# A pre-norm decoder layer with a sorted mixture of experts: another order of work at its start and in its last sorting

## The chip, the cores and the metric

The kernel runs on one core of a Trainium2 chip, as one program with one launch. The metric is device time in microseconds (us), the median of several runs. The core has a matrix engine (PE, TensorE), a vector engine (DVE), a scalar engine (ACT), a general engine (POOL, GpSimd) and SyncE (SP), which here only starts transfers. Each engine takes its instructions strictly in the order of the program; they wait for one another through semaphores. Transfers started by SP, ACT and POOL share 16 DMA engines. All data is fp32.

## The reference

There are 8 batches of 512 tokens with 256 features. Three blocks follow one another, each with a layer norm ahead and a residual add behind:

```python
# 1: attention as a causal circular convolution, 16 heads of 16
z = softmax(einsum('bse,he->bsh', x, W_A) * 16 ** -0.5, axis=1)
out[i] = sum over j <= i of z[(i - j) % S] * v[j]      # per head; then W_O and b_O
# 2: causal cross-attention: keys from norm(x), values and queries from ctx, scores / 16
# 3: mixture of experts: 2 shared experts of width 128 for all tokens,
#    16 routed experts of width 64, each token goes to the top 2 of a softmax router
out = shared(x) + sum over the 2 chosen e of weight_e * wd[e] @ (silu(wg[e] @ x) * (wu[e] @ x))
```

## The kernel before

**Batches and steps.** Work on a batch is cut into named steps, closures which issue their instructions when called. `steps_front` makes the first block's input side: `tr0 tr1` transpose the normed x, `z` makes the softmax over time (for batch 0 from two products, else by transposing), writes it to DRAM (`zd`) and loads it back as four shifted tiles `T`, 1 MB each; `v0 v1` make the values in time-reversed order, `q0 q1 cv0 cv1` the cross-attention's operands, `bias` adds b_O to x on POOL. `steps_back` makes the convolution (`c00` to `c11`, products `pc`), the projection, the second norm, scores, attention, third norm, and then the router: `lg` and `rt` (top 2), `rk` (the rank of each token in its expert: where its row goes), and eight sends `sd0` to `sd7`, indirect DMAs on POOL which write the token's row to its place in a DRAM table `xg` (line 584). `steps_shared` holds the shared experts: `h0 h1` (line 610, PSUM tag `gu` with three buffers) and `d0 d1` (line 627). A hand-written list `ORDER` interleaves the steps of the batches b-1 (names with `-`), b, b+1 (`+`) and b+2 (`++`).

**Routed experts.** The batches form two groups, 0 to 5 and 6 to 7. When a group's rows have been sent, each expert's rows lie together in `xg`, padded to tiles of 128 rows. `tiled` and `tabled` work out on DVE and PE which expert and which rows each tile has. The tiles are worked on in quads of four: group 0 has 16 quads, group 1 has 8. For a quad q, `fetch` loads the tiles' rows on SP (line 721), `pick` copies the expert's up and gate weights on ACT and loads the down weights `wdn`, `turn` transposes the rows (line 756; its first DVE operation, line 748, waits for the fetch), `hidden` makes the two products (line 775), `down` the third (line 791) and scales it, and four `put`s scatter the rows to a DRAM table `yg` by an indirect DMA on POOL (line 814). The fetch of quad 0 waits for the group's last send.

**Joining.** For each batch, `keep` reloads the saved x (group 0 only), `take` loads 2 x 512 KB from `yg` (line 858, on SP), and `join` adds both on DVE (line 867) and stores the output on SP. `yg` is one tensor in DRAM: the scatters to it are declared independent of each other, but a `take` waits for the scatters ahead of it in the program, and a scatter that the program has behind a `take` waits for this take.

**Order.** The order of issue comes from the program: `merged` spreads several lists evenly over each other, and `idle(n)` puts n empty steps in. The scheduler of the framework then moves instructions a little within each engine's queue. In iteration b=6 the first steps of group 0's tiles and quads 0 to 4 are spread over the iteration, in iteration 7 quads 5 to 12. Behind the loop come the last sorting (rank and sends of batch 7), the rest of group 0's quads and the shared experts of batch 7, in an order written out by hand; then group 1's quads, merged with the six joins of group 0 (`old`), and last the two joins of group 1. `warm` issues a product that nobody reads (128 x 128 by 512), behind each `hidden` and `down` of group 1.

Of the kernel before, what the change touches and what calls it, by code (L numbers as in the profile page):

```python
# [8 lines left out]
F32 = mybir.dt.float32  # L9
# [7 lines left out]
P = 128  # L17
B, S, D = 8, 512, 256
NT = S // P
KC = D // P  # L20
H, HD = 16, 16
NE = 16
MR = 64
# [49 lines left out]
def decoder_layer(ctx: ExitStack, tc: tile.TileContext, x, ctxT, waT, wvT, woT, bo, wkT, xwv, wqT, wr, wg, wu, wd, out):  # L73
    nc = tc.nc
# [16 lines left out]

    load_x(0)

    ident = const.tile([P, P], F32, name="ident")
    make_identity(nc, ident)
    mask = const.tile([P, P], F32, name="mask")
# [4 lines left out]
    nc.gpsimd.iota(rank_i, pattern=[[0, NT], [-1, NE]], base=NE, channel_multiplier=0)  # L101
    rank = const.tile([P, NT, NE], F32, name="rank")
    nc.vector.tensor_copy(rank, rank_i)
    ones = const.tile([P, P], F32, name="ones")
    nc.gpsimd.memset(ones, 1.0)

    before = const.tile([P, P], F32, name="before")
    nc.gpsimd.affine_select(out=before, in_=ones, compare_op=ALU.is_gt, fill=0.0, base=0, pattern=[[1, P]], channel_multiplier=-1)
# [163 lines left out]
    def steps_front(b):  # L272
        s = st[b]
# [11 lines left out]
        def zsoft():  # L285
            if b == 0:

                pz = ps.tile([P, 512], F32, tag="mm", bufs=3, name=f"pz{b}")
                for k in range(KC):
                    nc.tensor.matmul(pz[:H, :], wa_sb[:, k, :], s["xnT"][:, k, :], start=(k == 0), stop=(k == KC - 1))  # L290
                z = pz[:H, :].rearrange("h (i t) -> h i t", t=P)
            else:

                pz = ps.tile([P, 512], F32, tag="tr", bufs=2, name=f"pz{b}")
                for i in range(NT):
                    nc.tensor.transpose(pz[:H, i * P:(i + 1) * P], s["z"][:, i, :], ident)
                z = pz[:H, :].rearrange("h (i t) -> h i t", t=P)[:, :, ::-1]
            nm = small.tile([H, 1], F32, tag="znm", name=f"znm{b}")
            nc.vector.tensor_reduce(nm, pz[:H, :], AX.X, ALU.max, negate=True)
# [3 lines left out]
            nc.scalar.activation(zp[:, P:].rearrange("h (i t) -> h i t", t=P), z, AF.Exp, bias=nm, accum_out=zs)  # L303
            zr = small.tile([H, 1], F32, tag="zr", name=f"zr{b}")
            nc.vector.reciprocal(zr, zs)
            nc.vector.tensor_scalar_mul(zp[:, P:], zp[:, P:], zr)
            zd = dram.tile([H, ZW], F32, tag="zd", name=f"zd{b}")
            nc.sync.dma_start(out=zd, in_=zp)
            s["T"] = []
            for q in range(H // HPT):  # L310

                t = sb.tile([P, HPT, S], F32, tag="T", bufs=4, name=f"T{b}_{q}")
                src = bass.AP(zd.tensor, zd.offset + q * HPT * ZW + 1, [[1, P], [ZW, HPT], [1, S]])
                s["T_ins"] = nc.sync.dma_start(out=t, in_=src).ins
                s["T"].append(t)
            if 2 <= b < 6:
                for g in range(2):
                    put_blanks(g, b - 2, s["T_ins"])
# [316 lines left out]
        steps += [down(cp) for cp in range(2)]  # L635
        return named("h0 h1 d0 d1", steps)

    def warm(n, name, behind):

        p = ps.tile([P, 512], F32, tag="mm", bufs=3, name=f"warm_{name}")  # L640
        with tc.issue_after(behind):
            for _ in range(n):
                nc.tensor.matmul(p, ident, wgu_r[:, 0, 0, :512], start=True, stop=True)


    def tiled(g):

# [63 lines left out]
    def steps_routed(g):  # L711
# [53 lines left out]
        def hidden(q):  # L765
            def f():
                wgu, xT = G["wgu", q], G["xT", q]

                p = ps.tile([P, 2, QT // 2, P], F32, tag="gu", bufs=3, name=f"pgu{g}_{q}")
                for n in range(2):  # L770
                    for j in range(QT // 2):
                        for k in range(KC):
                            for o in range(2):
                                i = 2 * j + o
                                last = nc.tensor.matmul(p[o * MR:(o + 1) * MR, n, j, :], wgu[:, i, n, k, :], xT[:, k, i, :], start=(k == 0), stop=(k == KC - 1)).ins  # L775
                if g:
                    warm(1, f"h{q}", last)
                h = sb.tile([P, QT // 2, P], F32, tag="rh", bufs=2, name=f"rh{g}_{q}")
                nc.scalar.activation(h, p[:, 0], AF.Tanh, scale=0.5)
                nc.vector.scalar_tensor_tensor(h, h, 1.0, p[:, 0], ALU.add, ALU.mult)  # L780
                nc.vector.scalar_tensor_tensor(h, h, 0.5, p[:, 1], ALU.mult, ALU.mult)  # L781
                G["h", q] = h
            return f

        def down(q):
            def f():
                h, wdn = G["h", q], G["wdn", q]
                py = [ps.tile([P, QT // 2, D], F32, tag="gu", bufs=3, name=f"py{g}_{q}_{o}") for o in range(2)]
                for j in range(QT // 2):
                    for o in range(2):  # L790
                        last = nc.tensor.matmul(py[o][:, j, :], h[o * MR:(o + 1) * MR, j, :], wdn[o * MR:(o + 1) * MR, j, :], start=True, stop=True).ins  # L791
                if g:
                    warm(1, f"d{q}", last)
                if g == 0:
                    y = [sb.tile([P, D], F32, tag="y", bufs=8, name=f"y{g}_{q}_{i}") for i in range(QT)]
                else:
                    y = sb.tile([P, QT, D], F32, tag="xT", bufs=4, name=f"y{g}_{q}")
                    y = [y[:, i, :] for i in range(QT)]
                for o in range(2):
                    for j in range(QT // 2):  # L800
                        i = 2 * j + o
                        w = G["w", q][:, i:i + 1]
                        if j == 0:
                            nc.scalar.mul(y[i], py[o][:, j, :], w)  # L804
# [36 lines left out]
    def steps_join(g):  # L841
# [3 lines left out]
        def keep(bi):  # L845
            def f():
                b = GROUPS[g][bi]
                x = sb.tile([P, NT, D], F32, tag=("oT", "xn1", "ctxT")[bi % 3], bufs=1, name=f"xj{b}")
                nc.sync.dma_start(out=x, in_=st[b]["kept"])
                G["xj", bi] = x  # L850
            return f
# [30 lines left out]
    for n in FRONT.split():  # L882
        if n == "q0":
            make_qk()
        fronts[0][n]()
    for f in ln[1]:
        f()

    def iteration(b):
        x = dict(backs[b])  # L890
        if b > 0:
            x |= {f"-{n}": f for n, f in [*shared[b - 1].items(), *backs[b - 1].items()]}
        if b + 1 < B:
            x |= {f"+{n}": f for n, f in fronts[b + 1].items()}
        if b + 2 < B:
            x |= named("++l0 ++l1", ln[b + 2])

        ends = b == GROUPS[0][-1]
        order = ORDER.split() + (["rk", *[f"sd{i}" for i in range(8)]] if ends else [])
        return [x[n] for n in order if n in x and not (b == GROUPS[1][0] and n[:3] in ("-rk", "-sd"))]  # L900

    def flat(x):
        return [f for y in x for f in y]

    for b in range(B):
        if b + 2 < B:
            load_x(b + 2)
        now = iteration(b)
        if b == 6:
            now = merged(now, first[:1] + idle(4) + first[1:-1] + idle(12) + first[-1:] + flat(quads[:5]))  # L910
        elif b == 7:
            now = merged(now, flat(quads[5:13]))
        for f in now:
            f()
        if b == 0:
            load_blank()
        if b == 1:
            load_experts()
    last, sh = backs[B - 1], shared[B - 1]
    gap = flat(quads[13:])  # L920
    q = len(gap) // 4
    for f in [last["rk"], *gap[:q], sh["h0"], *[last[f"sd{i}"] for i in range(8)], *gap[q:2 * q], sh["h1"], first1[0],
              *gap[2 * q:3 * q], *first1[1:-1], *gap[3 * q:], sh["d0"], sh["d1"], first1[-1]]:
        f()
    keeps, takes, joins = steps_join(0)
    n = len(keeps)
    old = [keeps[0], takes[0], keeps[1], takes[1]]
    for i in range(n):
        old.append(joins[i])
        if i + 2 < n:  # L930
            old += [keeps[i + 2], takes[i + 2]]
    keeps, takes, joins = steps_join(1)
    for f in merged(flat(quads1), old):
        f()
    for f in [*keeps, *takes, *joins]:
        f()
# [54 lines left out]
```

## Time and profile before

| | |
|---|---|
| median of 3 runs | 583.35 us (580.09 to 584.81) |
| the profiled execution | 585.7 us; span of its instructions 584.0 us |
| busy: PE, DVE, ACT, POOL | 518.3, 373.7, 191.5, 228.1 us |
| mean granted PE clock | 0.966 |
| moved by DMA | 107.67 MB, mean 184 GB/s |

In the profile a line gives the start in us, the duration, the engine, the source line with the operation, what it writes and reads (partitions x elements), the number of instructions merged, and in brackets the engine's idle time ahead of it and what ended it. `128*64` ahead of a shape is the part of the PE array in use. An fp32 product shows as two records, a transpose as one. SPq, ACTq and POOLq are these engines' queues when they start transfers. A line of the waits reads: who waited for what: us in total, times, longest.

In time, the iterations of the loop fill about 30 to 478 us; the rank and the sends of batch 7 come from 478 to 493, group 1's quads from there to 562, and the last joins until 584.

### The profile page before, as it was taken

Reading aid. Unit: us, or ns where it says so; the run is one execution under the profiler, and the core shown is the slowest. Engines: PE = TensorE matmul, PEld = TensorE weight load, DVE = VectorE, ACT = ScalarE, POOL = GpSimd, SP = SyncE. Lnnn points to the kernel's source line nnn. Section 1 sums busy time; section 2 is a strip of 40 time slices with the busy share of each in tenths; the row PEclk is TensorE's granted clock in tenths of the full one; section 3 lists DMA queues with packets and bytes.
Section 4 is the critical chain, followed back from the end, with each engine's and each line's share of the span. In section 5 each row is a group of like instructions: output and inputs, shape, how many; then the busy total and the mean of one; then the engine's idle time right before and its main releaser. Section 6 shows DMA issues by size and latency. Waiting matters only on the chain.

```text
span 584.0 us, 10066 instructions
## 1 busy us (share of the span) xinstructions
PE 518.3 (89%) x3176; PEld 334.8 (57%) x3176; DVE 373.7 (64%) x1289; ACT 191.5 (33%) x483; POOL 228.1 (39%) x258
## 2 busy tenths in 40 slices
PE   3989989999999999999999679999899899898830
PEld 1537626666665675764765356775566665664510
DVE  4327848768768787877976476547756575453553
ACT  2233313322224233224222326444344342452310
POOL 3300302530540630621434402444576457564550
PEclk9999999999999999999999889999999999998985
DMA  8491090671391392184182357955556323778797
GB/s 272 143 396 34 11 347 23 200 279 58 139 348 59 111 324 110 66 305 192 48 293 98 109 153 193 313 165 199 164 171 207 101 88 123 197 231 298 229 327 251
DMA packets 64108, 107.67 MB, mean 184 GB/s; under 512 B 8902, under 2 KB 37580, under 8 KB 63954
## 3 DMA queue, kind: packets, MB, share of 16 engines
q1 hardware_dynamic: 51672, 83.87, 43.4%
q0 software_dynamic: 7680, 16.87, 8.0%
q10 hardware_dynamic: 4704, 6.29, 3.2%
q8 instruction: 25, 0.41, 0.3%
q14 instruction: 27, 0.22, 0.1%
HBM read 82.35 MB, written 34.38 MB: 200 GB/s over the span
## 4 chain that ended last, share of the span: by engine, by line
PE 54%; DMA 16%; DVE 11%; issue 6%; POOL 6%; SPq 3%; ACT 2%; ACTq 1%; POOLq 0%; DVEq 0%
PE pc L394 6%; DMA xs<-xg 5%; PE pgu L775 5%; PE pv L362 4%; PE psc L446 4%; DMA T<-zd 4%; PE pd L627 4%; PE pa L475 4%; PE pg L610 3%; PE pv L334 3%; PE pu L610 3%; PE po L428 3%; PE pt L252 3%; PE pq L350 3%; PE pxt L756 3%
## 5 line engine op out<-in xcount | busy, mean ns | idle before, releaser
L814 POOL DMA_INDIRECT yg<-y,to x96 | 96.8, 1008 | 91.7 <-ACT y L804 68.4
L236 POOL TENSOR_TENSOR rs<-ve,power 128x2 f32<-128x2 f32 x48 | 35.5, 747 | 188.1 <-DVE ve L235 187.8
L584 POOL DMA_INDIRECT xg<-row,place x64 | 63.3, 989 | 24.8 <-issue 17.1
L394 PE MATMUL pc<-T,vh 128*32 128x256 f32 (+1 forms) x512 | 56.9, 490 | 3.1 <-DMA T<-zd 1.6
L775 PE MATMUL pgu<-xsT,wgu 128*64 128x128 f32 x768 | 55.1, 282 | 0.3 <-DVE rh L781 0.3
L775 PEld LDWEIGHTS pgu<-xsT,wgu 128*64 128x64 f32 x768 | 43.9, 138 | 11.3 <-issue 7.0
L221 DVE BATCH_NORM_STATS2 bn<-x 128x6 f32<-128x256 f32 x96 | 37.7, 413 | 7.3 <-DMA x<-in_x_dram 6.3
L446 PE MATMUL psc<-kT,qT 128*128 128x128 f32 (+3 forms) x128 | 40.8, 441 | 0.7 <-DVE kT L257 0.7
L475 PE MATMUL pa<-v,pT 128*128 128x256 f32 x160 | 40.2, 382 | 0.7 <-DVE pT L466 0.7
L334 PE MATMUL pv<-wv_sb,xr 128*128 128x272 f32 (+1 forms) x128 | 36.5, 433 | 4.7 <-ACT xr L327 4.2
L394 PEld LDWEIGHTS pc<-T,vh 128*32 128x32 f32 x512 | 18.9, 109 | 32.1 <-issue 18.6
L610 PE MATMUL pg<-x2T,wg_sb 128*128 128x512 f32 x64 | 33.2, 626 | 3.3 <-DVE rh L781 2.3
L475 PEld LDWEIGHTS pa<-v,pT 128*128 128x128 f32 x160 | 29.2, 190 | 11.3 <-issue 3.6
L806 DVE TENSOR_SCALAR y<-py,w 128x256 f32<-128x256 f32 x48 | 22.4, 479 | 20.6 <-ACT y L804 17.7
L627 PE MATMUL pd<-wd_sb,h 128*128 128x256 f32 x128 | 33.6, 390 | 1.1 <-DVE y L806 0.8
L791 PE MATMUL py<-wdn,rh 64*128 64x256 f32 x192 | 30.9, 414 | 3.9 <-DMA wdn<-wdn_d 3.8
L428 PE MATMUL po<-wo_sb,oT 128*128 128x256 f32 x128 | 30.5, 392 | 4.3 <-DVE vh L339 4.3
L240 DVE TENSOR_SCALAR xn<-x,mv,rs 128x256 f32<-128x256 f32 x64 | 28.1, 476 | 9.4 <-POOL rs L236 7.6
L334 PEld LDWEIGHTS pv<-wv_sb,xr 128*128 128x128 f32 x128 | 26.1, 210 | 13.3 <-ACT xr L327 5.4
L252 PE MATMUL pt<-ident,xn 128*128 128x128 f32 x128 | 23.7, 292 | 10.8 <-DVE xn L240 8.3
L730 ACT COPY wgu<-wgu_r 128x256 f32 x96 | 32.0, 402 | 3.7 <-DVE oT L411 1.4
L756 PE MATMUL pxt<-ident,xs 128*128 128x128 f32 x192 | 29.3, 283 | 3.6 <-DMA xs<-xg 2.3
(176 smaller groups left out, 932.8 us busy)
## 6 DMA issues: line engine op xcount, KB each, us to landing
T<-zd SPq DMA_DIRECT2D x32, 1024.0 KB
xs<-xg SPq DMA_DIRECT2D x96, 129.0 KB
x<-in_x_dram SPq DMA_DIRECT2D x8, 512.0 KB
ctxT<-in_ctxT_dram SPq DMA_DIRECT2D x8, 512.0 KB
yj_qT<-yg SPq DMA_DIRECT2D x8, 512.0 KB
yj_v<-yg SPq DMA_DIRECT2D x8, 512.0 KB
xg<-blank SPq DMA_DIRECT2D x6, 516.0 KB
kept<-x ACTq DMA_DIRECT2D x6, 512.0 KB
```

The lines of the kernel that those rows point to most:

```text
L252: nc.tensor.transpose(pt[:, i * P:(i + 1) * P], xn[:, k * P:(k + 1) * P], ident)
L334: nc.tensor.matmul(pv[:, :w], xr[:, k, i, :], wv_sb[:, k, :w], start=(k == 0), stop=(k == KC - 1))
L394: nc.tensor.matmul(s["pc"][o][32 * g:32 * g + 32, 2 * jp * P:], vh[:, jp, h, :], s["T"][h // HPT][:, h % HPT, :S - 2 * jp * P], start=(jp ...
L428: nc.tensor.matmul(po[:, i, :], s["oT"][:, k, c * P:(c + 1) * P], wo_sb[:, k, :], start=(k == 0), stop=(k == KC - 1))
L446: nc.tensor.matmul(pc[:, :w], s["qT"][:, k, i * P:w], s["kT"][:, k, :w], start=(k == 0), stop=(k == KC - 1))
L475: nc.tensor.matmul(pa[:, :D], s["pT", i][:, j * P:(j + 1) * P], s["v2"][:, j, :], start=(j == 0), stop=(j == i))
L584: ins = nc.gpsimd.indirect_dma_start(out=grp[g]["xg"][:, :], out_offset=bass.IndirectOffsetOnAxis(ap=s["place"][:, r, c:c + 1], axis=0), i ...
L610: nc.tensor.matmul(p, w[:, k, mt * P:(mt + 1) * P], s["x2T"][:, k, :], start=(k == 0), stop=(k == KC - 1))
L627: nc.tensor.matmul(pd[:, i, :], s["h", mt][:, c * P:(c + 1) * P], wd_sb[:, mt, :], start=(mt == 0), stop=(mt == NSH - 1))
L756: nc.tensor.transpose(pt[:, i * P:(i + 1) * P], xs[:, i, 2 + k * P:2 + (k + 1) * P], ident)
L775: last = nc.tensor.matmul(p[o * MR:(o + 1) * MR, n, j, :], wgu[:, i, n, k, :], xT[:, k, i, :], start=(k == 0), stop=(k == KC - 1)).ins
L814: ins = nc.gpsimd.indirect_dma_start(out=G["yg"][:, :], out_offset=bass.IndirectOffsetOnAxis(ap=G["to", q][:, i:i + 1], axis=0), in_=G["y" ...
```

## The change

It changes the order of work at the start, which batch's shared experts lie where, and the unread products:

- `ones` is set on DVE instead of POOL at the very start, and 14 unread products of `ones` with itself are issued on PE ahead of everything else. The function `warm` and its 16 products in group 1 are gone.
- The first norm of batch 1 (`ln[1]`) is issued behind the DVE instruction which scales batch 0's `zp`.
- In iteration 6, 22 instead of 12 empty steps stand ahead of the first `turn`, and quads 0 to 5 are in it instead of 0 to 4; iteration 7 has quads 6 to 13.
- The shared experts of batch 6 are no longer in iteration 7. They come in the last sorting, with those of batch 7.
- The last sorting is now a merge of three lists: rank, sends and the first steps of group 1's tiles; quads 14 and on with both batches' shared experts; and the first five steps of the joins of group 0 (keep 0, take 0, keep 1, take 1, join 0). The order which results has take 0 in the middle of the last scatters of group 0, and take 1 ahead of the very last.
- The buffers of the kept x are used in another order (`xn1`, `ctxT`, `oT`).

```diff
     load_x(0)
+    ones = const.tile([P, P], F32, name="ones")
+    nc.vector.memset(ones, 1.0)
+
+    idle_p = ps.tile([P, 512], F32, tag="mm", bufs=3, name="idle_p")
+    for i in range(14):
+        nc.tensor.matmul(idle_p[:, :P], ones, ones, start=True, stop=True)
...
-    ones = const.tile([P, P], F32, name="ones")
-    nc.gpsimd.memset(ones, 1.0)
...
-            nc.vector.tensor_scalar_mul(zp[:, P:], zp[:, P:], zr)
+            s["zp_ins"] = nc.vector.tensor_scalar_mul(zp[:, P:], zp[:, P:], zr).ins
...
-    def warm(n, name, behind):
-
-        p = ps.tile([P, 512], F32, tag="mm", bufs=3, name=f"warm_{name}")
-        with tc.issue_after(behind):
-            for _ in range(n):
-                nc.tensor.matmul(p, ident, wgu_r[:, 0, 0, :512], start=True, stop=True)
...
-                if g:
-                    warm(1, f"h{q}", last)
...
-                if g:
-                    warm(1, f"d{q}", last)
...
-                x = sb.tile([P, NT, D], F32, tag=("oT", "xn1", "ctxT")[bi % 3], bufs=1, name=f"xj{b}")
+                x = sb.tile([P, NT, D], F32, tag=("xn1", "ctxT", "oT")[bi % 3], bufs=1, name=f"xj{b}")
...
-    for f in ln[1]:
-        f()
+    with tc.issue_after(st[0]["zp_ins"]):
+        for f in ln[1]:
+            f()
...
-        return [x[n] for n in order if n in x and not (b == GROUPS[1][0] and n[:3] in ("-rk", "-sd"))]
+        late = ("-h0", "-h1", "-d0", "-d1") if b == B - 1 else ()
+        return [x[n] for n in order if n in x and n not in late and not (b == GROUPS[1][0] and n[:3] in ("-rk", "-sd"))]
...
         if b == 6:
-            now = merged(now, first[:1] + idle(4) + first[1:-1] + idle(12) + first[-1:] + flat(quads[:5]))
+            now = merged(now, first[:1] + idle(4) + first[1:-1] + idle(22) + first[-1:] + flat(quads[:6]))
         elif b == 7:
-            now = merged(now, flat(quads[5:13]))
+            now = merged(now, flat(quads[6:14]))
...
-    last, sh = backs[B - 1], shared[B - 1]
-    gap = flat(quads[13:])
-    q = len(gap) // 4
-    for f in [last["rk"], *gap[:q], sh["h0"], *[last[f"sd{i}"] for i in range(8)], *gap[q:2 * q], sh["h1"], first1[0],
-              *gap[2 * q:3 * q], *first1[1:-1], *gap[3 * q:], sh["d0"], sh["d1"], first1[-1]]:
-        f()
+    last, sh6, sh7 = backs[B - 1], shared[B - 2], shared[B - 1]
+    send = [last[f"sd{i}"] for i in range(8)]
+    gap = flat(quads[14:])
+    sh = [x[n] for x in (sh6, sh7) for n in ("h0", "h1", "d0", "d1")]
+    sorting = [last["rk"], *idle(3), *send, first1[0], *idle(0), *first1[1:-1], *idle(2), first1[-1]]
+    for f in merged(sorting, gap + sh, [*idle(0), *old[:5]]):
+        f()
     keeps, takes, joins = steps_join(1)
-    for f in merged(flat(quads1), old):
+    for f in merged(flat(quads1), old[5:]):
         f()
```

The list `old` is unchanged (keeps, takes and joins of batches 0 to 5, in turn); it is now made ahead of the loop.

More of the change, by code (lines that the diff above doesn't have):

```diff
@@ L774, in f @@
                                 i = 2 * j + o
-                                last = nc.tensor.matmul(p[o * MR:(o + 1) * MR, n, j, :], wgu[:, i, n, k, :], xT[:, k, i, :], start=(k == 0), stop=(k == KC - 1)).ins
-                if g:
-                    warm(1, f"h{q}", last)
+                                nc.tensor.matmul(p[o * MR:(o + 1) * MR, n, j, :], wgu[:, i, n, k, :], xT[:, k, i, :], start=(k == 0), stop=(k == KC - 1))
                 h = sb.tile([P, QT // 2, P], F32, tag="rh", bufs=2, name=f"rh{g}_{q}")
@@ L790, in f @@
                     for o in range(2):
-                        last = nc.tensor.matmul(py[o][:, j, :], h[o * MR:(o + 1) * MR, j, :], wdn[o * MR:(o + 1) * MR, j, :], start=True, stop=True).ins
-                if g:
-                    warm(1, f"d{q}", last)
+                        nc.tensor.matmul(py[o][:, j, :], h[o * MR:(o + 1) * MR, j, :], wdn[o * MR:(o + 1) * MR, j, :], start=True, stop=True)
                 if g == 0:
@@ L899, in iteration @@
         order = ORDER.split() + (["rk", *[f"sd{i}" for i in range(8)]] if ends else [])
-        return [x[n] for n in order if n in x and not (b == GROUPS[1][0] and n[:3] in ("-rk", "-sd"))]
+        late = ("-h0", "-h1", "-d0", "-d1") if b == B - 1 else ()
+        return [x[n] for n in order if n in x and n not in late and not (b == GROUPS[1][0] and n[:3] in ("-rk", "-sd"))]
     def flat(x):
         return [f for y in x for f in y]
[L905 to L909, printed above, removed]
-            now = merged(now, first[:1] + idle(4) + first[1:-1] + idle(12) + first[-1:] + flat(quads[:5]))
-        elif b == 7:
-            now = merged(now, flat(quads[5:13]))
-        for f in now:
-            f()
[L915 to L918, printed above, removed]
-    last, sh = backs[B - 1], shared[B - 1]
-    gap = flat(quads[13:])
-    q = len(gap) // 4
-    for f in [last["rk"], *gap[:q], sh["h0"], *[last[f"sd{i}"] for i in range(8)], *gap[q:2 * q], sh["h1"], first1[0],
-              *gap[2 * q:3 * q], *first1[1:-1], *gap[3 * q:], sh["d0"], sh["d1"], first1[-1]]:
-        f()
     keeps, takes, joins = steps_join(0)
@@ L931, in decoder_layer @@
             old += [keeps[i + 2], takes[i + 2]]
+    for b in range(B):
+        if b + 2 < B:
+            load_x(b + 2)
+        now = iteration(b)
+        if b == 6:
+            now = merged(now, first[:1] + idle(4) + first[1:-1] + idle(22) + first[-1:] + flat(quads[:6]))
+        elif b == 7:
+            now = merged(now, flat(quads[6:14]))
+        for f in now:
+            f()
+        if b == 0:
+            load_blank()
+        if b == 1:
+            load_experts()
+    last, sh6, sh7 = backs[B - 1], shared[B - 2], shared[B - 1]
[4 more added lines that the diff above has]
+    for f in merged(sorting, gap + sh, [*idle(0), *old[:5]]):
+        f()
     keeps, takes, joins = steps_join(1)
-    for f in merged(flat(quads1), old):
+    for f in merged(flat(quads1), old[5:]):
         f()
```

## The prediction

> **What bounds the kernel now.** I read the stage table first (busy time of PE, PEld, DVE, ACT, POOL in each stretch, then granted PE clock, DMA share, GB/s):
>
> ```profile
> 440.00:460.00 20.00, 19.08 (x133) 14.00 (x134) 13.63 (x40) 8.61 (x23) 11.62 (x14) 1.00 0.51 160
> 480.00:500.00 20.00, 18.20 (x133) 12.15 (x131) 12.36 (x52) 6.53 (x16) 15.12 (x17) 1.00 0.44 143
> 500.00:520.00 20.00, 19.17 (x164) 12.65 (x166) 9.04 (x26) 10.22 (x27) 10.90 (x12) 1.00 0.66 201
> 520.00:540.00 20.00, 17.34 (x131) 10.51 (x128) 9.31 (x19) 6.55 (x17) 11.15 (x11) 0.86 0.85 280
> 560.00:584.00 24.00, 1.79 (x9) 0.63 (x5) 10.49 (x10) 0.84 (x2) 6.54 (x6) 0.61 0.77 274
> ```
>
> Up to about 500 us the PE is full and the DMA has room. From 500 on a good part of the PE's busy time is unread products, the DMA is close to what it ever moves, and after 562 the PE is done. Next, the first 40 us in order of time:
>
> ```profile
> 11.69 0.75 DVE L221 BATCH_NORM_STATS2 bn<-x 128x6 f32<-128x256 f32 x2 [1.92 <-DMA x<-in_x_dram]
> 13.15 0.41 DVE L257 COPY xnT<-pt 128x256 f32<-128x256 f32 x1
> 13.61 1.89 PE L290 MATMUL pz<-xnT,wv_sb 128*16 128x512 f32 x2 [0.83 <-DVE xnT L257]
> 15.42 3.71 PE L334 MATMUL pv<-wv_sb,xr 128*128 128x256 f32 x8
> 18.13 0.67 DVE L299 TENSOR_REDUCE znm<-pz 16x1 f32<-16x512 f32 x1
> 19.66 1.99 PE L334 MATMUL pv<-wv_sb,xr 128*128 128x256 f32 x8 [0.52 <-ACT zp L303]
> ```
>
> DVE waits for the second x and measures it (L221) ahead of the copy that batch 0's z needs; the reduction of z (L299) starts 2.6 us after pz ends, behind the norm of batch 1. The same eight products cost 3.71, then 1.99: the PE is at half clock until about 17. Last, POOL in the tail, and the PE there:
>
> ```profile
> 490.85 0.96 POOL L584 DMA_INDIRECT xg<-row,place  x1 [0.30 <-issue]
> 506.22 0.97 POOL L814 DMA_INDIRECT yg<-y,to  x1 [0.30 <-DVE rh L780]
> 513.25 0.97 POOL L814 DMA_INDIRECT yg<-y,to  x1 [6.05 <-ACT y L804]
> 543.35 0.97 POOL L814 DMA_INDIRECT yg<-y,to  x1 [8.30 <-ACT y L804]
> 566.72 1.35 POOL L814 DMA_INDIRECT yg<-y,to  x1 [0.30 <-issue]
> ```
> ```profile
> 521.31 1.12 PE L643 MATMUL warm_h<-wgu_r,ident 128*128 128x512 f32 x2
> 534.04 0.44 PE L756 MATMUL pxt<-ident,xs 128*128 128x128 f32 x2 [2.33 <-DMA xs<-xg]
> 539.61 1.89 PE L643 MATMUL warm_h<-wgu_r,ident 128*128 128x512 f32 x2
> ```
>
> The last send of batch 7 starts at 490.85; group 1's 32 scatters run from 513.25 to 568.07, each at least 1.28 us after the last (0.98 + 0.30): 41 us of work in 54.8. Four takes, joins and stores fill the 16 us to 584.
>
> **Start.** ones moves to DVE and 14 unread products (28 records) run before the first transpose at 7.24: at most 28 x 0.215 = 6.0 us (a 128-wide record costs half of the 0.43 that pz's and pv's cold records suggest), in idle PE time, cost nothing. With batch 1's norm behind zp, the copy of 13.15 comes at 10.9, pz's second half at 12.8 instead of 13.6, and L299 directly behind it. If the clock is still halved: pz ends at 14.7, zp is scaled at about 16.5 instead of 19.99 and without POOL's bias beside it (1.83 us there), zd leaves 4.7 us earlier, and the PE goes pv, pqk, pq, pv2 without the 0.52 and 0.83 waits: pc begins at 29 instead of 30.9; T's last quarter, which holds pc at 39.15, is no longer late. Gain 3.4. With a warm clock pz and pv lose another 0.8 + 1.7: 5.7. Here a rule bears: the Trainium skill, "TensorE: Matmul & The Clock Gate", Part 4, says transposes don't count as PE-busy in the usual way, and between 7.2 and 10.9 there are only eight transposes. The nearest row agrees that sparse transposes (324 to 327.7) are followed by pv at 3.64 us. I take **-4.0**. From 100 to 280 the PE is 99% busy, so this is carried to iteration 6.
>
> **Iterations 6 and 7.** The slots for the first tiles move from 12 to 22 idles, but in the two instruction lists the DVE read of the first xs (L748, the 8.9 us wait at 337) keeps its neighbours, so PE's 4.3 us stall there stays: 0. Iteration 6 takes one quad more. Batch 6's shared experts leave iteration 7: 1.98+1.88+3.43+1.88 (L610) and 1.97+2.44 (L627) = 13.6 us of PE. One quad more (pxt 1.04, pgu 1.97, py 1.13) ahead of the router: +4.1. Its three scatters must now go ahead of the sends: from batch 6's first send (418.98) to batch 7's (481.98) POOL has to do 35 DMAs x 1.28 + 4.5 = 49.5 us; the PE would leave 50, so I add 2 for a queue that can't be packed full. Batch 7's first send (call it T) moves from 482 by -4 -13.6 +4.1 +2 = **-11.5** to 470.5.
>
> **The last sorting.** Here waits are added, and this speaks against the change. In the new POOL queue seven sends are followed by put(13,3), which must wait for take(0), since take reads the rows that it writes; then three puts, and only then the eighth send, on which every fetch of group 1 waits. take(0) leaves at T+1 (its put's landing 2.4), lands about T+7 (before: 4.7 to 6.8 for the pair); seven sends end at T+8.9: no stall, but for each us that it lands later all behind it is later. The eighth send starts at T+14 instead of T+8.9 and lands at T+17.5. SP then has fetch 0, take(1), fetches 1 to 3 in that order; take(1) waits for put(15,2), landed T+22.6, so fetches 1 to 3 leave after T+23.6 and land behind its 1 MB from T+29.
>
> DVE is in order too: y of tile 15,3 waits for put(13,3) to land (T+12.4), and the tables of group 1 (ptab on PE, then 15.5 us of shared experts) queue behind it: the PE idles from T+3 to T+13. Later join(1) waits for take(1) (T+29) ahead of batch 7's shared activation, which frees the PSUM slot of the fourth hidden product: at T+30.4. From there: product 2 to 3, the rest of the down products 4 to 5, pxt, pgu, pxt, pgu, py 7 to 9; the first put of group 1 at T+46, where before it came at T+31. So **+15**: the first put at 516.5 instead of 513.25. At best (take(1) and its join out of the way) PE work alone gives T+37, that is +6; at worst T+55.
>
> **Tail without warm.** Before, quads come every 5.95 us (512.4, 518.5, 524.4); 16 unread products of some 1 us each go, and a quad is 4.1 us of PE, under POOL's 5.12. That gives 4 x 0.83 = 3.3. Of POOL's remaining idle (8.3 at 543, 2.8 at 557, 0.8: for xs and wdn) about half goes, because two takes and one store (2.5 MB; 9 us at 268 GB/s, the 19 MB that move in 513 to 584) have left the tail: 6. A warm product at half clock (1.89 at 539.61) behind a late fetch also goes; it lies inside the 6. What can't go: 41 us of POOL. **-9.5**, between -3 and -13.
>
> A second rule speaks against it: the same page's table "Why this matters for your kernels" wants no PE gap over about 3 us. By it gaps of 5.1 - 4.1 = 1 us cost nothing. The row is harsher (2.33 us of gap at 534.04, half clock until 541.5), but shows nothing for a gap of 1.2 (440.68). At half clock a quad is 7.5 us, over 5.12, and then the PE is full and warms up again. I take 0 for the pace; a permanent half clock would cost 7 x 2.4 = 17.
>
> **Sum.** -11.5 + 15 - 9.5 = -6.0, last 16 us unchanged; moved memsets and other buffers for keeps lie under loads: 0. Profiled: 585.7 us (span 584.0), so 579.7. The median of the runs shown is 583.35, 2.35 lower: 577.4, and I write 577.0, as the 1.4 of the scaling at 19.99 are only half in it.
>
> **Rivals.**
> 1. *The sorting doesn't hold anything up* (first put at T+37): -15, 568. For it: DMA share is only 0.44 there, takes are free. Against: three in-order queues each have a take ahead of group 1. 0.2.
> 2. *Slower: the takes in POOL's and SP's queues decide.* If take(0) lands 5 us after the seventh send, the eighth send, and with take(1) as late, the first put comes at T+55 (525): +12 - 3 (tail still DMA-bound) = +9, 592. It decides from a first put later than about 523 on. Against: the DMA share of 0.44. 0.2.
> 3. *The end is DMA-bound*: what is left in the tail stays at 268 GB/s, scatters stretch to 52 us, 0 to -3: 582. Speaks for it: share 0.85. 0.2.
> 4. My sum: 0.4.
>
> A measurement here tells about 1% from no change. Faster by over 1% (below 577.5): rival 1 and somewhat over half of mine and the edges, 0.5; within 1%: 0.28; slower: 0.22. My own case lies in 572 to 582; with the rivals' ends 565 to 592.
>
> **What would show it.** L299 near 15 and pc near 29 at the start; pv at 2 or 3.7 tells the clock. The first send of batch 7 near 470, the first group 1 put near 516, PE idle about 10 us before ptab, quads 5.1 us apart afterwards. Wrong if the put(13,3) waits for long on DMA, if quads are 6 or more apart, or if the PE clock stays halved past 520.

## The result and the profile after

The changed kernel takes **575.41 us** (median of 4 runs, 574.3 to 575.89), the kernel before on the same occasion 582.12 us (580.09 to 584.81): ratio **0.9885**, 95% interval 0.985 to 0.992, that is -6.7 us. The forecast was 577.0. The profiled execution took 575.53 us with a span of 573.8; the one before had 584.0. Executions of one kernel differ by some 3 us to either side (the kernel with the new start alone: 572.53 to 578.25 in six runs), so the 10.2 us between the two traces are not the 6.7 us between the medians: sizes of a part come below from medians, places from traces. Ratios leave out runs that were marked as slow, so a ratio can differ a little from the quotient of two medians.

The stage table of the changed kernel (busy time of PE, PEld, DVE, ACT, POOL in each stretch, then granted PE clock, DMA share, GB/s):

```profile
440.00:460.00 20.00, 17.81 (x143) 12.82 (x145) 10.72 (x34) 8.46 (x22) 12.16 (x14) 0.91 0.24 79
480.00:500.00 20.00, 17.35 (x45) 9.26 (x46) 9.39 (x22) 4.44 (x11) 8.08 (x8) 0.84 0.60 177
500.00:520.00 20.00, 19.29 (x207) 16.55 (x205) 11.96 (x29) 9.69 (x25) 5.80 (x5) 0.96 0.61 190
520.00:540.00 20.00, 13.76 (x142) 10.11 (x140) 10.16 (x23) 9.09 (x24) 15.43 (x16) 0.89 0.93 290
540.00:560.00 20.00, 8.98 (x56) 6.70 (x53) 7.92 (x12) 2.90 (x7) 14.29 (x13) 0.59 0.74 248
```

The last of these stretches in the kernel before:

```profile
540.00:560.00 20.00, 16.20 (x113) 9.52 (x114) 10.85 (x19) 5.41 (x14) 10.62 (x11) 0.97 0.81 263
```

Three things differ from before. The sorting (480 to 500) now has the shared experts of two batches, 45 long PE instructions instead of 133. The end (520 to 560) has 23 us of PE work instead of 34, and in its first half POOL is at 15.4 of 20 and the DMA share at 0.93. And the PE clock is 0.59 from 540 to 560, where it was 0.97.

The start, PE and DVE together in order of time (line numbers are 4 higher than before up to line 630):

```profile
7.13 0.44 PE L256 MATMUL pt<-ident,xn 128*128 128x128 f32 x2
10.25 3.46 PE L294 MATMUL pz<-xnT,wv_sb 128*16 128x512 f32 x4 [0.24 <-ACT xnT L259]
13.64 3.72 PE L338 MATMUL pv<-wv_sb,xr 128*128 128x256 f32 x16
13.75 0.68 DVE L303 TENSOR_REDUCE znm<-pz 16x1 f32<-16x512 f32 x1 [3.28 <-PE pz L294]
15.62 0.80 DVE L310 TENSOR_SCALAR zp<-zp,zr 16x512 f32<-16x512 f32 x1
16.55 0.41 DVE L225 BATCH_NORM_STATS2 bn<-x 128x6 f32<-128x256 f32 x1
34.55 2.77 PE L398 MATMUL pc<-T,vh 128*32 128x512 f32 x24 [0.23 <-DMA T<-zd]
```

The reduction of z follows pz at once, 4.4 us earlier than before (18.13); the norm of batch 1 stands behind zp; the last wait for T ends at 34.55 instead of 39.15. All sixteen pv records take 3.72 us, where before eight took that: the clock is full from 13.6 on (granted clock 1.00 from 13.6 to 15.4). pz is still at half clock (granted clock 0.50 from 10.25 to 12). In the kernel before, this row shows 1.00 in the same stretch although its pz records are no faster (1.89 for two, here 3.46 for four), so at the start the durations are the surer sign.

The last sorting on POOL's queue:

```profile
466.93 0.97 POOL L588 DMA_INDIRECT xg<-row,place  x1 [1.83 <-DVE row L579]
...
476.00 0.96 POOL L588 DMA_INDIRECT xg<-row,place  x1 [0.31 <-issue]
477.27 0.99 POOL L807 DMA_INDIRECT yg<-y,to  x1 [0.30 <-DMA xg<-row,place]
...
482.42 0.97 POOL L588 DMA_INDIRECT xg<-row,place  x1 [0.30 <-issue]
...
495.62 1.39 POOL L807 DMA_INDIRECT yg<-y,to  x1 [7.09 <-DMA yj_v<-yg]
512.98 0.97 POOL L807 DMA_INDIRECT yg<-y,to  x1 [15.97 <-ACT y L797]
...
558.55 0.97 POOL L807 DMA_INDIRECT yg<-y,to  x1 [0.30 <-issue]
```

and the PE's waits there and in the tail:

```profile
473.54 1.12 PE L614 MATMUL pg<-x2T,wg_sb 128*128 128x512 f32 x2 [1.54 <-DVE h L618]
480.03 0.37 PE L697 MATMUL ptab<-ident,row 128*1 128x128 f32 x1 [5.37 <-DVE row L685]
496.81 2.50 PE L614 MATMUL pu<-x2T,wu_sb 128*128 128x512 f32 x4 [2.63 <-DVE h L618]
539.46 2.23 PE L786 MATMUL py<-wdn,rh 64*128 64x256 f32 x8 [1.19 <-DMA wdn<-wdn_d]
549.20 2.28 PE L786 MATMUL py<-wdn,rh 64*128 64x256 f32 x8 [2.50 <-DMA wdn<-wdn_d]
```

The first send of batch 7 (T) is at 466.93 instead of 481.98. Seven sends, four scatters, then the eighth send at T+15.5. The first of these scatters lands late for DVE, which waits 5.86 us for it until 479.42; the `row` for which ptab waits (L685) stands directly behind, at 479.82. The last scatter of group 0 waits 7.09 us for take 1. The first scatter of group 1 comes at T+46.05 (before T+31.3), the last at 558.55. The two py lines of the tail are at half clock (2.2 instead of 1.13).

### The profile page after: what moved, and what is told of

Same layout as the page of the kernel before. It is cut to its first block, busy times and chain, and to the rows that moved or that the text cites. A ratio compares the mean times of both kernels' runs of the same rounds, so it can differ in the third digit from the quotient of the medians.

```text
span 573.8 us, 10065 instructions
## 1 busy us (share of the span) xinstructions
PE 508.6 (89%) x3172; PEld 337.0 (59%) x3172; DVE 370.1 (64%) x1290; ACT 190.6 (33%) x483; POOL 231.7 (40%) x257
## 4 chain that ended last, share of the span: by engine, by line
PE 52%; DMA 17%; DVE 13%; POOL 7%; issue 5%; ACT 2%; SPq 2%; POOLq 0%; ACTq 0%; DVEq 0%
PE pc L398 6%; PE pd L631 4%; PE psc L450 4%; PE pa L479 4%; DMA T<-zd 4%; PE pgu L772 4%; PE pv L366 4%; PE pu L614 3%; PE pt L256 3%; PE pq L354 3%; POOL yg L807 3%; PE pv L338 3%; PE pg L614 3%; DMA xg<-row,place 3%; DMA yg<-y,to 3%
## 5 line engine op out<-in xcount | busy, mean ns | idle before, releaser
L807 POOL DMA_INDIRECT yg<-y,to x96 | 99.2, 1033 | 84.3 <-ACT y L797 50.3
L588 POOL DMA_INDIRECT xg<-row,place x64 | 64.7, 1011 | 26.4 <-issue 16.2
L398 PE MATMUL pc<-T,vh 128*32 128x256 f32 (+1 forms) x512 | 58.1, 490 | 3.1 <-DMA T<-zd 1.6
L772 PE MATMUL pgu<-xsT,wgu 128*64 128x128 f32 x768 | 54.4, 284 | 2.6 <-DVE rh L776 2.1
L479 PE MATMUL pa<-v,pT 128*128 128x256 f32 x160 | 42.1, 394 | 0.0
L338 PE MATMUL pv<-wv_sb,xr 128*128 128x272 f32 (+1 forms) x128 | 34.1, 413 | 4.2 <-ACT xr L331 4.2
L786 PE MATMUL py<-wdn,rh 64*128 64x256 f32 x192 | 32.5, 428 | 5.7 <-DMA wdn<-wdn_d 4.9
L614 PE MATMUL pu<-x2T,wu_sb 128*128 128x512 f32 x64 | 32.0, 621 | 2.6 <-DVE h L618 2.6
L338 PEld LDWEIGHTS pv<-wv_sb,xr 128*128 128x128 f32 x128 | 24.8, 199 | 11.4 <-ACT xr L331 5.4
```

What stands on the lines that cost most here:

```text
L338: nc.tensor.matmul(pv[:, :w], xr[:, k, i, :], wv_sb[:, k, :w], start=(k == 0), stop=(k == KC - 1))
L398: nc.tensor.matmul(s["pc"][o][32 * g:32 * g + 32, 2 * jp * P:], vh[:, jp, h, :], s["T"][h // HPT][:, h % HPT, :S - 2 * jp * P], start=(jp ...
L479: nc.tensor.matmul(pa[:, :D], s["pT", i][:, j * P:(j + 1) * P], s["v2"][:, j, :], start=(j == 0), stop=(j == i))
L588: ins = nc.gpsimd.indirect_dma_start(out=grp[g]["xg"][:, :], out_offset=bass.IndirectOffsetOnAxis(ap=s["place"][:, r, c:c + 1], axis=0), i ...
L614: nc.tensor.matmul(p, w[:, k, mt * P:(mt + 1) * P], s["x2T"][:, k, :], start=(k == 0), stop=(k == KC - 1))
L807: ins = nc.gpsimd.indirect_dma_start(out=G["yg"][:, :], out_offset=bass.IndirectOffsetOnAxis(ap=G["to", q][:, i:i + 1], axis=0), in_=G["y" ...
```

## The experiments

Each ratio is against the kernel before on the same chip.

**The new start alone.** This is the kernel before with three parts of the change: `ones` on DVE at the very start, the 14 unread products ahead of everything, and `ln[1]` behind `zp`.

> The kernel before with only the new start (ones on DVE, 14 unread products, batch 1's first norm behind zp). My theory: the 4.6 us that the changed kernel has won when pc's last quarter of batch 0 starts (39.15 to 34.55) is carried by a full PE through all iterations, so the whole time falls by about 4.5 us, ratio 0.992. Rival: the tail is held by transfers and scatters and gives the lead back; then the ratio is 1.000 although the last sends are 4.5 us earlier.

Measured: 575.6 us, ratio **0.9879** (0.9835 to 0.9922), -7.0 us, more than the 4.5 expected, with an interval (-9.6 to -4.5) that just leaves 4.5 in. This part alone gives as much as the whole change. Its trace shows how the gain is carried: the rank product `pk` of the batches 0 to 5 starts

| batch | 0 | 1 | 2 | 3 | 4 | 5 |
|---|---|---|---|---|---|---|
| before | 87.58 | 137.62 | 184.69 | 230.86 | 277.02 | 316.80 |
| new start | 83.18 | 133.21 | 180.28 | 226.44 | 272.59 | 312.37 |

4.4 us earlier each time, nothing lost on the way. Between 325 and 345 another 2 us comes in: the stall of PE ahead of the second `po` is 1.49 us instead of 4.29, and at T the trace is 8.9 us ahead (473.05). What brings in the rest up to T is not shown.

**The changed kernel with the old start** (the same edit, undone):

> The changed kernel with the start of before. My theory: all comes 4.6 us later, ratio to the kernel before 0.996. Rival: the wait of POOL and SP for take 0 and take 1 or the transfers of the tail absorb it, ratio 0.9885 as with the new start.

Measured: 581.57 us, ratio **0.9989** (0.9965 to 1.0013), -0.6 us. So all the rest of the change together (shared experts, sorting, takes, no unread products at the end) is worth about nothing. In its trace T is at 471.52, 10.5 us ahead of before, and the first scatter of group 1 at 516.71, 3.5 us behind before: what T gains, the sorting takes. (The spans of these two traces, 577.0 and 584.0, are 7.0 us apart where the medians show 0.6 to 0.9: one execution lies low among its runs and the other high.)

**The kernel before without its 16 unread products in group 1** (only the two calls of `warm` removed):

> The kernel before with only the 16 unread products of group 1 taken out. My theory: quads of group 1 come every 5.2 us instead of 5.95 until transfers are late, 3 to 4 us less in all, ratio 0.994. Rival 1: the DMA bounds the tail, ratio 1.000. Rival 2 (clock): without them the PE is at half clock for most of the tail, quads take 6 us or more, ratio over 1.005.

Measured: 580.91 us, ratio 0.9969 (0.9945 to 0.9993), -1.8 us instead of the 3 to 4 expected; the time from group 1's first scatter to its last is 51.7 us instead of 53.5.

**The changed kernel with these 16 products back:**

> The changed kernel with the 16 unread products of group 1 put back. My theory: as the first scatter of group 1 stays near 513 and quads go back to 5.95 us, it is 3 to 6 us slower than the changed kernel, ratio to the kernel before 0.995 to 0.999. Rival (clock): they keep the clock up at 535 to 560, where the changed kernel has 0.59, and so cost nothing or win 1 to 2 us.

Measured: 576.49 us, ratio 0.9901 (0.9865 to 0.9937), which is 0.9 us more than the changed kernel, with overlapping intervals; 3 to 6 were expected. First to last scatter 46.6 us, against 45.6 without the products. Without them the second and third quad take 5.13 and 5.12 us instead of 5.95 each, but later quads then wait for their transfers, and 1.0 us is left. The products are thus the small part of what the tail lost (1 to 1.8 us). The large part, 53.5 to 46.6, is mostly one wait of POOL for a quad, 8.30 us before (the line at 543.35) and this in the changed kernel:

```profile
542.29 0.97 POOL L807 DMA_INDIRECT yg<-y,to  x1 [1.82 <-ACT y L797]
```

Two takes and a store have left this tail; whether they are the cause, the runs with other places of the takes tell only in part.

The next four ran on a chip on which the kernel before takes 620.76 us; what is different there is told in the last section.

**The start without its 14 unread products** (order alone):

```diff
-    idle_p = ps.tile([P, 512], F32, tag="mm", bufs=3, name="idle_p")
-    for i in range(14):
-        nc.tensor.matmul(idle_p[:, :P], ones, ones, start=True, stop=True)
```

> The kernel before with the new order at the start (second norm behind batch 0's first z, ones on DVE), without the 14 unread products. Theory A (order is what counts): the copy of xnT comes 2 us earlier and the reduction of z follows at once; pz and pv stay at half clock (3.5 and 3.7 us for 8 records), pc's last quarter comes 3.4 us earlier, so about 578.5, ratio 0.994, and the rest of start_only's 7 us belongs to the clock. Theory B (the unread products only fill idle PE time): pv at half clock costs nothing, since pc waits for zp and zd and not for pv: 575.5, ratio 0.988, as with both. If the products are all of it: 582, ratio 1.000.

Measured: ratio **0.9917** (0.9892 to 0.9941), -5.2 us. The first 40 us of its trace:

```profile
7.05 0.69 PE L253 MATMUL pt<-ident,xn 128*128 128x128 f32 x2 [7.05 <-DVE xn L241]
10.44 3.60 PE L291 MATMUL pz<-xnT,wv_sb 128*16 128x512 f32 x4
13.97 3.77 PE L335 MATMUL pv<-wv_sb,xr 128*128 128x256 f32 x16
14.08 0.68 DVE L300 TENSOR_REDUCE znm<-pz 16x1 f32<-16x512 f32 x1 [3.21 <-PE pz L291]
34.45 2.77 PE L395 MATMUL pc<-T,vh 128*32 128x512 f32 x24 [0.38 <-DMA T<-zd]
```

This is the start of the changed kernel, to 0.3 us, without any product ahead of it: pz at half clock, pv at full clock, the last wait for T over at 34.45 (34.55 with the products), the first `pk` at 82.67 (82.58 with the products, on the same chip). The products make the transposes quicker (0.44 instead of 0.69 a pair), but these wait for DVE anyway. So what the start has gained by 83 us is the order. By the time, the interval holds theory A's 0.994 and not theory B's 0.988; but 0.988 came from another chip, and here the kernel with the products, which is the next, is no faster to within the intervals. Its trace is 1.70 us ahead at the `pk` of batch 5 (312.56, order alone 314.26); whether the products do this is not shown.

**The new start, and no unread products at the end** (both edits on the kernel before):

> The kernel before with the whole new start and without the 16 unread products at the end; the last sorting, the shared experts and the takes as before. If the two gains add (start 0.9879, products 0.9969): 0.985, 573.6 us, faster than the whole change (0.9885). If the earlier start makes the end bound by its transfers, so that the products no longer cost anything: 0.988, 575.4.

Measured there: ratio 0.9907 (0.9881 to 0.9932), not distinguishable from the order alone; neither forecast lies in the interval (0.985, and 0.988 only just outside).

**The changed kernel with the takes back in the tail:**

```diff
-    for f in merged(sorting, gap + sh, [*idle(0), *old[:5]]):
+    for f in merged(sorting, gap + sh):
...
-    for f in merged(flat(quads1), old[5:]):
+    for f in merged(flat(quads1), old):
```

> The kernel after, with the two takes, keeps and the join of group 0 that it puts into the last sorting back in the tail. Theory of the prediction: without take(0) ahead of put(13,3) and take(1) ahead of the fetches of group 1 the first put of group 1 comes at T+37 instead of T+46 (T: first send of batch 7), but 2.5 MB return to the tail, which gives back up to 6 us: first put near 504, end 571 to 576, ratio 0.982 to 0.989. Rival (sorting and tail are bound by what they move, wherever the takes stand): first put earlier, last put unchanged at 558, 575.4 us, ratio 0.9885, nothing gained. Second rival (the shared experts of batches 6 and 7, 27 us of PE, set the first put and not the takes): first put stays within 2 us of T+46, and with the takes in the tail the end is later: 578 or more.

Measured: ratio 0.9919 (0.9896 to 0.9942), slower than the first two forecasts. T is at 503.11, ptab follows at T+4.8, the first scatter of group 1 at T+42.2, and from there to the last are 54.4 us. On this chip the sorting of the kernel before (with the new start, no products) also takes T+42.3 and its tail 55.7 us, so nothing can be told from this about what the takes gain or lose; the changed kernel itself did not run on this chip.

**The changed kernel with the takes five slots later:**

```diff
-    for f in merged(sorting, gap + sh, [*idle(0), *old[:5]]):
+    for f in merged(sorting, gap + sh, [*idle(5), *old[:5]]):
```

> The kernel after, with the same takes, keeps and join in the last sorting but five slots later, so that more of the sends and fetches are issued ahead of them. If the takes' place in the in-order queues decides: first put of group 1 at T+38 to T+42, and the two takes still out of the tail: 569 to 572, ratio 0.978 to 0.983. If it is the shared experts' PE time: first put at T+46 as in the kernel after, ratio 0.9885.

Measured: ratio 0.9856 (0.9793 to 0.9919), an interval that holds the first forecast (0.978 to 0.983) in part and the rival's 0.9885 as well: inconclusive by time. ptab comes at T+5.0, the first scatter of group 1 at T+41.3. From there to the last are 54.7 us, against 54.4 in the run above, which has the two takes in the tail: on this chip the tail is no shorter without them.

The last four ran on a chip on which the kernel before takes 582.86 us.

**The first tiles' reads held back.** In the kernel before, DVE waits for the first fetch of group 0 with the PE behind it:

```profile
337.07 0.16 DVE L748 TENSOR_TENSOR to<-xs,far 128x4 int32<-128x4 f32 x1 [8.94 <-DMA xs<-xg]
338.96 3.00 PE L428 MATMUL po<-wo_sb,oT 128*128 128x256 f32 x8 [4.29 <-DVE vh L339]
```

The edit puts these reads behind the vh copies for which the PE waits:

```diff
-                nc.vector.tensor_tensor(G["to", q], xs[:, :, 0], ...)
+                with tc.issue_after(st[7]["vh", 0]) if (g, q) == (0, 0) else nullcontext():
+                    nc.vector.tensor_tensor(G["to", q], xs[:, :, 0], ...)
...            # the same for w
-                    nc.vector.tensor_copy(vh[:, jp, 1::2, ...], src[:, :, 1])
+                    s["vh", jp] = nc.vector.tensor_copy(vh[:, jp, 1::2, ...], src[:, :, 1]).ins
```

> The kernel before, with the two small DVE reads of group 0's first tiles (to and w) held back behind the vh copies of batch 7's first half, so that DVE no longer waits for the fetch (8.9 us until 337.07) ahead of them. Theory A (the extra 3 to 4 us that start_only gained between 325 and 345 is this stall of the PE, 4.29 us, with the half clock behind it): the second po starts near 334.7 at full clock, gain 4.3 to 7, ratio 0.988 to 0.993. Theory B (the stall only moves: what comes behind it waits for the same fetch): 582, ratio 1.000.

Measured: 582.06 us, ratio **0.9982** (0.9952 to 1.0011). Its trace at that place:

```profile
333.06 4.77 PE L428 MATMUL po<-wo_sb,oT 128*128 128x256 f32 x16
336.80 0.16 DVE L749 TENSOR_TENSOR to<-xs,far 128x4 int32<-128x4 f32 x1 [2.69 <-DMA xs<-xg]
339.83 1.19 PE L334 MATMUL pv<-wv_sb,xr 128*128 128x272 f32 x4 [1.08 <-DVE x L430]
```

The stall is gone (both halves of `po` run together), 1.08 us of it comes back at the next pv, and T is 4.4 us earlier in the trace (477.61). By the ratio 1.1 us of this reaches the end, at most 2.8, and the interval includes none at all, as theory B said.

**The new start with the same reads held back:**

> The kernel before with the whole new start and the same two reads held back. Theory A (start_only has already lost most of that stall, 1.49 us are left): 0 to 1.5 us under start_only, ratio 0.985 to 0.988. Theory B (start_only's extra gain came from somewhere else, so both gains add): 0.0120 + 0.007 to 0.012, ratio 0.976 to 0.981.

Measured: 576.58 us, ratio 0.9878 (0.9843 to 0.9913). Beside the new start's 0.9879, measured on another chip, the edit gives nothing, as theory A said.

**The new start without the products at the end, on this chip:**

> The kernel before with the whole new start and without the 16 unread products at the end, once more, beside start_turn_late, which has the products. If the products cost their 1.6 us here too: 0.985, under start_turn_late without its share of the stall. If the earlier start has made the end bound by its transfers: 0.988.

Measured: **573.13 us, ratio 0.9826** (0.979 to 0.9863): the sum of the two single effects (0.9848) lies in the interval. This is the lowest time of all kernels tried, with the sorting, the shared experts and the takes as they were before. Its lead over the changed kernel (0.9885) is not certain, since the two intervals overlap, and the slower chip did not show it.

**The changed kernel with late takes and the reads held back:**

> The kernel after with its takes, keeps and join five slots later in the last sorting and with the two reads of the first tiles held back. If the takes' place in the in-order queues decides: ptab without the 5.4 us stall of the PE, first put of group 1 at T+38 to T+42 (T: first send of batch 7; after: T+46), and about 4 us of it reach the end: 570, ratio 0.979 to 0.983. If the shared experts of two batches hold the PE anyway: T+46 and ratio 0.987.

Measured: 574.18 us, ratio 0.988 (0.9843 to 0.9916). PE and POOL in its sorting, whose first send is at 468.06:

```profile
469.71 0.27 PE L697 MATMUL ptab<-ident,row 128*1 128x128 f32 x1
484.35 0.96 PE L755 MATMUL pxt<-ident,xs 128*128 128x128 f32 x2 [8.78 <-DMA xs<-xg]
508.36 0.97 POOL L809 DMA_INDIRECT yg<-y,to  x1 [13.61 <-ACT y L799]
```

ptab comes at T+1.7 instead of T+13.1: the 5.4 us stall goes with the place of take 0. The first scatter of group 1 follows at T+40.3 instead of T+46.05, as the first theory said, but the time is the rival's. But the PE now waits 8.78 us for the first fetch behind the eighth send, while some 15 us of the shared experts' products stand behind this transposition in its queue; an order with them ahead of it was not tried. The last scatter comes at 556.0, only 2.6 us earlier, and POOL waits longer for a quad in the tail, although the same two takes have left it:

```profile
540.15 0.97 POOL L809 DMA_INDIRECT yg<-y,to  x1 [4.82 <-ACT y L799]
```

So the changed kernel's short wait of 1.82 us is not due to the takes alone. From the first scatter to the last are 47.6 us here and 50.4 in the run above on the same chip, which has the takes in its tail: 2.8 us, where the comparison further up gave 6.9.

## Why the prediction was right

Its total (577.0) is 1.6 us off, and its sum of -6.0 is near the -6.7 between the medians. The parts are less good than the sum: it had -4 for the start and -2 for the rest; the runs alone say -7.0 (-9.6 to -4.5) and -0.6 (-2.0 to +0.8). That the total is so near is in part luck. In the traces, in which the prediction did its sum, the parts add up to -10.2 (-15.05 at T, +14.8 in the sorting, -8.3 in the tail, -1.65 behind it), and not to -6.0: the ledger alone (579.7) was 4.2 us above the execution that was profiled after. The 2.35 which the prediction took off because the profiled execution before was a long one made most of this good.

- **Start, -4.0.** Right in place and nearly in size: 4.4 to 4.6 us are carried from 34 us to 316 us without loss, because the PE is full there. The line of the reduction was expected near 15 and stands at 13.75, pc near 29 and stands at 25.91; of that, 4.6 us reach the last wait for T. The two cases of the clock (3.4 halved, 5.7 warm) were both wrong in detail: pz is at half clock and pv is warm, with and without the 14 products. The rule on transposes was rightly given weight: after 6.00 us of unread products the transposes run at full speed (0.44), and after three microseconds with only eight sparse transposes pz is at half speed again. Whether that is because they are transposes or because they are sparse, no run separates. In the kernel before, half clock lasts through all eight pv records, to about 19 and not 17.
- **Iteration 6, "the 4.3 stall stays: 0".** This step failed. The stall was 4.29 us before, and again without the 16 products; it is shorter in the changed kernel and in two traces of the new start without the change's other parts (1.03, 1.49 and 2.99, the lines below). With everything but the start it is 1.89. The argument looked at DVE's order, which is indeed unchanged, but the stall's length depends on when the fetch is issued, and that moved: in the kernel before the SP queue issues it 4.2 us after the last send starts (328.78 to 333.02), in the changed kernel 3.2 us (323.81 to 326.96), with the new start alone 2.4 us (324.36 to 326.80). Why it is issued sooner was not tried. Little of the stall reaches the end. Holding the reads back alone gave -1.1 us; and on one chip the new start is at T at 474.53 with the reads held back and at 474.50 without, with 2.99 us of stall. So the 4.4 to 4.6 us that are carried are at the edge of the start's interval (-9.6 to -4.5), and what it gains beyond them has no cause shown.

```profile
332.92 1.99 PE L432 MATMUL po<-wo_sb,oT 128*128 128x256 f32 x8 [1.03 <-DVE vh L343]
332.68 2.00 PE L432 MATMUL po<-wo_sb,oT 128*128 128x256 f32 x8 [1.49 <-DVE vh L343]
333.14 1.99 PE L432 MATMUL po<-wo_sb,oT 128*128 128x256 f32 x8 [2.99 <-DVE vh L343]
```

- **Shared experts and the quad more, -11.5 at T.** Measured in the trace -15.05: the start's 4.6 (changed kernel against the one with the old start, 471.52 to 466.93), and 10.5 for the rest where 7.5 was forecast. Of these 3 us, 2 are the shorter stall (second `po` at 337.00 instead of 338.96).
- **The last sorting, +15.** Forecast T+46, measured T+46.05, and the chain was the one named: the eighth send at T+15.5 (forecast T+14), the first fetch issued at T+18, take 1 at T+22.9 (22.6), the next fetches at T+24.2 (23.6), the PE idle 1.5 and 5.4 us ahead of ptab (forecast some 10 in all), h of batch 7 behind join 1 at T+29.2 (30.4). take 0 holds up nothing on POOL, as assumed. Issuing the takes later, on another chip, took 5.7 of the 15 us away and showed that a fetch behind the eighth send is what comes next.
- **The tail, -9.5.** From the first scatter to the end of the last, 54.8 became 46.5: -8.3. The two terms were 3.3 for the products' pace and 6 for the takes. The pace fell as forecast (5.95 to 5.12 for a quad), but only 1 to 1.8 us of it are left at the last scatter, because later quads wait for their transfers: the term was too big. All eight quads start 5.1 to 7.3 us apart, 5.9 in the mean, where 5.1 was expected. For the takes the traces give 6.9 in the first comparison and 2.8 in the second, both with other differences beside the takes, and nothing on the slower chip (54.4 and 54.7): how much of the tail is theirs stays open.
- **The clock in the tail, 0.** The prediction named a clock halved past 520 as a sign of being wrong; it is 0.89 from 520 to 540 and 0.59 from 540 to 560. Its second rule, by which gaps of the PE under about 3 us cost no clock, did not hold here: the longest wait of the PE from 520 to its last product is 2.50 us, and the granted clock was already 0.57 from 535 to 540, behind a wait of 1.73. The time was right nevertheless, for the reason given in the same place: POOL's queue is packed. From 543 to 559 its scatters wait some 0.30 us each, although py takes 2.28 us instead of 1.13.
- **The last 16 us unchanged.** They came out at 14.3 in this execution (559.5 to 573.8). Before, two stores of group 0's joins start in or just ahead of this stretch (564.32 and 569.53), now the last of them start at 549.73; that this is the cause was not tried.
- **Rivals.** That the sorting holds nothing up (first scatter at T+37) is excluded by T+46.05. That the takes decide and make it slower is half true: they cost 5.7 us there, take 0 stalls no scatter, and the ratio is below 1. That the end is bound by its transfers is wrong in its size (the scatters take 46.5 us and not 52) but has something in it: with the takes late, at a DMA share of 0.93 from 520 to 540, a first scatter 4.6 us earlier brought the last one only 2.6 us forward, and no time that the medians can tell. The prediction's reading that the DMA, at 280 GB/s, was close to what it ever moves was not right: from 4 to 17 us the same trace shows 322 GB/s. The move of the shared experts and takes pays with 15 us in the sorting for what it gains before and after it.

## What to carry to other kernels

Here one engine was full for hundreds of microseconds, and the 4.4 us by which its first long-lived input (the tiles T, through one small reduction that stood behind a norm nobody needed yet) came earlier were still there 280 us later. Where a kernel looks like this, look at its start before the crowded end. A reordering that moves work into an in-order queue is paid for at everything behind it: write out the queue, and expect that when one wait is moved away the next one (here the fetch behind the last send) stands just behind. Check a change of several parts by undoing one part on the same chip, since the traces of single executions here differed by more than most parts are worth.

## What was not expected of the hardware

One kernel (the new start, no products at the end) ran on two chips: 573.13 us on one, 614.91 on the other, each with its kernel before in step (582.86 and 620.76). The two traces agree to 0.9 us up to 312.6 us (`pk` of batch 5 at 312.58 and 312.56). Then they part, in the routed stages; T is at 474.50 and 498.01. The stretch in which they do so most, on the slower chip:

```profile
420.00:440.00 20.00, 11.67 (x60) 7.22 (x61) 5.01 (x15) 4.40 (x12) 10.63 (x12) 0.76 0.34 110
```

and on the other:

```profile
420.00:440.00 20.00, 17.54 (x165) 12.84 (x163) 10.58 (x31) 9.75 (x28) 13.88 (x15) 1.00 0.56 175
```

On the slower chip the PE is busy for 11.67 instead of 17.54 us there and DVE and ACT for less than half the time, with a DMA share of 0.34 instead of 0.56. Its SP queue takes 4.83 us for a fetch of four tiles at 423.34, where the other takes 1.93 at 427.42, and at 430 PE, ACT and DVE come out of a pause of 3 to 6 us together:

```profile
430.10 0.81 PE L760 MATMUL pxt<-ident,xs 128*128 128x128 f32 x4 [3.31 <-issue]
431.14 0.74 DVE L244 TENSOR_SCALAR xn<-x,mv,rs 128x256 f32<-128x256 f32 x2 [5.52 <-PE pxt L760]
```

The profile shows nothing for which the PE waited in these 3.31 us; what holds the engines there stays open. The first 83 us are not touched by it, so the start's gain can be read on either chip; the sizes of the parts after 320 us can't be carried from one to the other.

The other surprise is how little the 14 products at the start do for the PE clock: they ran for 6.00 us, nearly all of it at half speed (0.21 us for a record), and by the time the first long product came, the clock was down again.
